# The fifth chunk of the keys as 15 block products, in pairs of half-width tiles, among the queries' products

## The chip, the core and the metric

One NeuronCore of a Trainium2 chip runs the whole kernel in one launch. The metric is device time in microseconds, the median of several runs. Everything is float32.

The engines are TensorE (PE in the profile, with its weight loads as PEld), VectorE (DVE), ScalarE (ACT), GpSimd (POOL) and SyncE (SP, which starts most DMAs). TensorE writes its products to PSUM, and VectorE and ScalarE read them from there. Each engine takes its own instructions in order and waits for the others by semaphores.

## The reference

A cross-attention block over 16 batches, each with 100 queries of width 640 and 718 keys of width 384 (plus four more tokens), in 8 heads of 80. Cut to what matters:

```
query = hidden_states @ Wq
keyt  = enc @ Wk
valt  = enc @ Wv
hs    = _mha(query, keyt, valt)              # softmax(q k^T / sqrt(80)) v, 8 heads
ca_hs1 = _mha(ca_q1, residual, residual)     # the four tokens' attention
ca_hs2 = _mha(ca_hs1 @ Wq, ca @ Wk_ca, ca @ Wv_ca)
out = (hs + ca_hs2) @ Wout + b_out + residual
```

The change concerns `keyt = enc @ Wk`: 718 keys from 384 inputs to 640 outputs. The 640 outputs stand in five chunks of 128 rows.

## The kernel before

**Batches.** `tile_xattn_kernel` loops over 16 batches. In turn `b` it finishes the attention of batch `b`, makes the values of `b` (`Values`, L410) and the keys of `b + 1` (`Keys`, L453), and prepares the second attention of `b + 1` and `b + 2` (`Second`, L854). Instructions are placed in the order of the program on each engine (`manual_schedule`). Parts that have steps of their own, `Keys`, `Values` and the softmax's `Maximum` (L785), are moved on by calls of `go(n)` in an order written by hand.

**Keys by 15 block products.** A product of 3 x 3 blocks by 3 x 2 blocks would take 18 block products. `Keys` and `Values` take 15: each multiplies a sum of input blocks by a sum of weight blocks, and the results collect in five accumulators A to E. After each product the accumulator is read and added to an output block, and the next product adds to the accumulator where it stands. `V_PLAN` and `K_PLAN` list (accumulator, form, output block); a form is the number of a pair of sums. The sums of the inputs are made on POOL for each batch (`enc_sums`, L481, 13 operations), those of the weights once (`weight_sums`, L502, 12 operations). The first write to an output block is a ScalarE copy (L407), later ones are VectorE additions (L405).

**The fifth chunk.** `Keys` makes chunks 0 to 3 of the 640 outputs in twos. The fifth, chunk 4, is left over and is made plainly: `last_keys` (L685) calls `chunk_keys` (L662), nine products of 128 x 128 weights with 240 columns each (L667), and two ScalarE copies (L678). It stands after the last block products of the turn, once VectorE has subtracted the maximum (`subtract(2)`, L1375) and ScalarE has the last exponential (L1383) in its queue.

**Queries.** Queries are made for two batches at a time, so in odd turns. In turns 3, 5, 7, 9, 11 and 13 the class `Queries` (L559) makes them by block products: `sums` puts six sums on POOL (L588), `make` (L607) first makes the fifth chunk of the queries (L626), then the others in pairs of column tiles of 64 (`product`, L590: weights of 64 columns, once for output partitions 0 to 63 and once for 64 to 127, matmul L594). Its accumulators a to e are read by ScalarE (L639, L647, L653, L655) and VectorE (L622). After it come the attention products (L1589), the products for the second attention (L875), and the next batch's scores (L710).

**Output pairs.** In five turns (last batch in `PAIRS`: turns 3, 6, 8, 11, 13) `project_pair` (L1144) makes two tiles of the output between `last_keys` and the queries. So turns 3, 11 and 13 have both, and turns 5, 7 and 9 have queries without an output pair (`parted`).

**The second attention** of four tokens runs beside this: `scores1` (POOL, L902 and L909), `softmax1` (a `Maximum` on VectorE; L801, L803, L806, L813, L831, L921), `scores2` (whose last step is L972 on POOL), `exponentials2` (ScalarE, L978), `softmax3`, `values2` (POOL, L1001 and L1008, token by token), and `keys` (POOL, L846), which masks the tokens' keys for `products` (L875).

**PSUM.** Three pools: `ps2` (two pairs of banks), `psk` and `ps1` (two banks each). `last_keys` took a pair from `ps2`.

**The largest of the scores** collects in `most`, a constant tile: 120 rows by `larger` (L1387, L1399), while rows 96 to 127 had been set to a low number once.

## Time and profile before

| | |
|---|---|
| median of 3 runs | 917.08 us (916.9 to 917.73) |
| the profiled execution's own time | 916.04 us |
| its span, first to last instruction | 914.1 us |
| granted TensorE clock | 1.000 |
| TensorE busy | 908.2 us, 99% |
| VectorE, ScalarE, POOL busy | 699.0, 434.2, 706.8 us |

The profile page gives busy time for each engine, groups of instructions by line, and waits; the timeline gives instructions in order of time, with the start, the length (of the whole row, where a row stands for several) and in brackets the idle time before and what ended it. A row such as `L594 ... x16` stands for 16 records. One float32 matmul leaves two records. TensorE's lengths overlap, since matmuls are pipelined: the time that a group takes is best read from its start to the start of the next.

### The profile page before, as it was taken

How to read it: one execution, taken by the hardware profiler on the slowest of the kernel's cores; microseconds unless marked ns; L12 is line 12 of the kernel's file. 1: busy time of each engine (PE TensorE's matmuls, PEld its weight loads, DVE VectorE, ACT ScalarE, POOL GpSimd, SP SyncE). 2: the span in 40 equal slices, each digit the busy share in tenths (PEclk: the TensorE clock that was granted, in tenths of full speed). 3: DMA queues.
4: the chain of work that ended last, by engine and by line, in shares of the span. 5: the costliest groups of instructions: out<-in, count | busy, mean ns of one | idle time of the engine just before them, and what ended most of it. 6: DMA issues, size and time to landing. Idle time of an engine off the chain costs nothing.

```text
span 914.1 us, 27711 instructions
## 1 busy us (share of the span) xinstructions
PE 908.2 (99%) x11962; PEld 762.8 (83%) x11962; DVE 699.0 (76%) x1126; ACT 434.2 (47%) x834; POOL 706.8 (77%) x672
## 2 busy tenths in 40 slices
PE   9999999999999999999999999999999999999998
PEld 6988889797797979888798787988879788797866
DVE  3669795989759897785967869679785897748883
ACT  2244543736337363652727436274741737427341
POOL 8577999787958879696896959958797697976623
PEclk9999999999999999999999999999999999999999
DMA  8822111131301212130121301103120031210111
GB/s 269 294 75 63 47 47 53 37 94 52 96 18 50 80 38 69 55 104 32 51 56 54 105 32 52 55 25 105 54 82 32 25 106 53 82 46 24 61 45 39
DMA packets 50582, 62.94 MB, mean 69 GB/s; under 512 B 13682, under 2 KB 37810, under 8 KB 50460
## 3 DMA queue, kind: packets, MB, share of 16 engines
q1 hardware_dynamic: 48812, 59.18, 21.2%
q8 instruction: 94, 1.54, 0.7%
q10 hardware_dynamic: 1024, 1.15, 0.4%
q0 software_dynamic: 624, 0.85, 0.3%
q14 instruction: 28, 0.23, 0.1%
HBM read 55.59 MB, written 5.57 MB: 67 GB/s over the span
## 4 chain that ended last, share of the span: by engine, by line
PE 96%; DVE 3%; ACT 0%; issue 0%; DVEq 0%
PE a_ps L1589 12%; PE s_ps L710 12%; PE v_psA L434 11%; PE v_psB L434 9%; PE k_psA L465 8%; PE k_psB L465 7%; PE kT_ps L667 6%; PE o_ps L1161 5%; PE v_psC L434 4%; PE k_psC L465 3%; PE q_ps L594 2%; PE q_ps L536 2%; PE v_psE L434 2%; PE v_psD L434 2%; PE v_ps L375 2%; PE q_psA L594 1%
## 5 line engine op out<-in xcount | busy, mean ns | idle before, releaser
L902 POOL TENSOR_TENSOR e<-ca,g 100x800 f32<-100x800 f32 x64 | 99.3, 1562 | 107.0 <-ACT kT L407 78.5
L500 POOL TENSOR_TENSOR enc<-enc 128x240 f32<-128x240 f32 x144 | 113.3, 797 | 14.7 <-DMA enc<-in_enct 7.5
L1375 DVE TENSOR_TENSOR st<-st,over 120x1600 f32<-120x1600 f32 x48 | 114.9, 2395 | 0.0
L1589 PEld LDWEIGHTS a_ps<-vs,st 120*36 120x36 f32 (+3 forms) x3072 | 109.3, 124 | 3.5 <-issue 3.4
L1589 PE MATMUL a_ps<-vs,st 120*36 120x81 f32 (+3 forms) x3072 | 111.7, 233 | 0.0
L434 PE MATMUL v_psA<-wv_sb,enc 128*120 128x320 f32 x352 | 109.3, 433 | 0.0
L1008 POOL TENSOR_TENSOR hs<-hs,hs 100x640 f32<-100x640 f32 x48 | 94.8, 1974 | 3.8
L1001 POOL TENSOR_TENSOR hs<-vb,p 100x640 f32<-100x640 f32 x64 | 91.1, 1434 | 8.4 <-issue 4.7
L465 PE MATMUL k_psA<-enc,wk_sb 128*128 128x240 f32 x384 | 95.3, 371 | 0.1
L909 POOL TENSOR_TENSOR e<-e,e 100x800 f32<-100x800 f32 x48 | 91.8, 1913 | 3.8
L434 PE MATMUL v_psB<-wv_sb,enc 128*120 128x320 f32 x296 | 91.8, 433 | 0.0
L1383 ACT ACTIVATE st<-st 120x1600 f32<-120x1600 f32 x48 | 73.9, 1539 | 32.3 <-DVE st L1375 31.8
L465 PEld LDWEIGHTS k_psA<-enc,wk_sb 128*128 128x128 f32 x384 | 71.5, 190 | 16.3 <-DVE wk_sb L522 0.5
L434 PEld LDWEIGHTS v_psA<-wv_sb,enc 128*120 128x120 f32 x352 | 64.2, 183 | 25.0 <-DVE vs L405 0.5
L1387 DVE TENSOR_TENSOR most<-most,st 120x800 f32<-120x800 f32 x64 | 66.3, 1036 | 15.9 <-ACT st L760 14.7
L465 PE MATMUL k_psB<-enc,wk_sb 128*128 128x240 f32 x320 | 78.0, 366 | 0.3 <-DVE sm L983 0.3
L710 PE MATMUL s_ps<-qp,kT 64*56 64x100 f32 (+1 forms) x3072 | 73.1, 248 | 0.0
L434 PEld LDWEIGHTS v_psB<-wv_sb,enc 128*120 128x120 f32 x296 | 54.1, 183 | 21.9 <-DVE vs L405 0.4
L710 PEld LDWEIGHTS s_ps<-qp,kT 64*56 64x56 f32 (+1 forms) x3072 | 66.9, 130 | 5.4 <-issue 4.2
L1076 ACT COPY hsT<-turned_hs 32x160 f32<-32x160 f32 (+7 forms) x244 | 67.7, 277 | 3.0
L465 PEld LDWEIGHTS k_psB<-enc,wk_sb 128*128 128x128 f32 x320 | 60.7, 190 | 8.6 <-issue 0.7
L766 ACT COPY st<-s_ps 120x800 f32<-120x800 f32 x64 | 49.8, 829 | 33.6 <-PE s_ps L710 33.6
(196 smaller groups left out, 1824.6 us busy)
## 6 DMA issues: line engine op xcount, KB each, us to landing
vb<-va_d SPq DMA_DIRECT2D x62, 250.0 KB
enc<-in_enct SPq DMA_DIRECT2D x30, 240.0 KB
enc<-in_enct SPq DMA_DIRECT2D x15, 360.0 KB
xT<-in_xt SPq DMA_DIRECT2D x8, 500.0 KB
rest<-in_enct SPq DMA_DIRECT2D x31, 120.0 KB
xn<-in_x SPq DMA_DIRECT2D x11, 320.0 KB
out<-xn SPq DMA_DIRECT2D x11, 320.0 KB
ca<-in_cas SPq DMA_DIRECT2D x16, 156.2 KB
```

Of the source, the lines that this page charges most:

```text
L434: nc.tensor.matmul(at[0][j][:KN, : H // 2], a_form(self.enc, f)[:, j * KN : (j + 1) * KN], wv_there.get(f, wv_sb[:, W_AT[f]]), start=first ...
L465: nc.tensor.matmul(at[:, i * KT : (i + 1) * KT], wk_sb[:, W_AT[f], i], a_form(self.enc, f), start=(first and i == 0), stop=last, skip_grou ...
L500: nc.gpsimd.tensor_tensor(out, left, right, op)
L710: nc.tensor.matmul(s_ps[at][k0:k1, cols], w, rhs, start=not begun & {(at, k) for k in range(k0, k1, 32)}, stop=last, skip_group_check=True,)
L902: first = nc.gpsimd.tensor_tensor(to, self.ca[:, t, :].unsqueeze(1).to_broadcast([S, NH, S]), g[:, :, t].unsqueeze(2).to_broadcast([S, NH, ...
L909: nc.gpsimd.tensor_tensor(e, e, to, ALU.add)
L1001: first = nc.gpsimd.tensor_tensor(to, self.vb[t][:S].rearrange("p (h d) -> p h d", h=NH), p2[:, :, t].unsqueeze(2).to_broadcast([S, NH, D] ...
L1008: nc.gpsimd.tensor_tensor(sums, sums, to, ALU.add)
L1076: nc.scalar.copy(self.hsT(r)[32 * m : 32 * m + 32, :, first - lo : end - lo], turned[32 * i : 32 * i + 32, :, m, first - at : end - at],)
L1375: return nc.vector.tensor_tensor(st[i], st[i], top.over[:KN].unsqueeze(1).to_broadcast([KN, 2, ROWS]), ALU.subtract,)
L1383: nc.scalar.activation(st[i], st[i], AF.Exp, scale=SCALE)
L1589: nc.tensor.matmul(a_v[lo:hi, h % 4], st[i // 2][: KEYS[i], i % 2, h * S + lo : h * S + hi], block(i, h // 4)[: KEYS[i], h % 4], start=(i ...
```

## The change

In turns 3, 5, 7, 9, 11 and 13 (`MIXED`) chunk 4 of the next batch's keys is no longer made by `last_keys`. A new class `Chunk` makes it by the same 15 forms, with weight blocks of 64 columns (`w4_form`: twelve sums in `w4_sums`, made by POOL in turn 1, and three blocks of `wk4` itself).

The products run in eight steps (`K4_PLAN`). Seven steps are a pair: two forms at a time, one to partitions 0 to 63 and one to 64 to 127, each streaming its own 240 input columns. One step is D alone, as two halves of 120 columns. A and B share one `ps1` bank, C, D and E another. After each step its two results are read: the first write to an output block by ScalarE, later ones by VectorE. The steps stand among the queries' products in `make`: two ahead, then one after each of the fifth chunk, a, b and so on.

With it go some moves. `softmax1` of these turns is cut into finer steps (`fine`) that stand between the queries' products or, where there is an output pair, between its products. The fourth token of `values2` and the masks `keys` move behind the queries' POOL step (the former already stood behind `sums` in turns 5, 7 and 9). `most` moves from a constant tile to one of the two `wide` buffers, and its rows from 96 on are set by a ScalarE copy in every batch.

```diff
+K4_PLAN = [
+    [("A", 7, (2, 1)), ("B", 13, (1, 0))],
+    [("D", 1, (2, 0))],
+    [("E", 6, (1, 0)), ("C", 12, (0, 1))],
+    [("A", 3, (2, 0)), ("B", 8, (2, 0))],
+    [("A", 9, (1, 0)), ("B", 10, (2, 1))],
+    [("A", 2, (0, 0)), ("B", 4, (0, 1))],
+    [("A", 0, (0, 1)), ("C", 11, (2, 1))],
+    [("A", 5, (1, 1)), ("B", 14, (0, 0))],
+]
...
         def make(self, tiles, chunk, between, freed):
...
+            chunk.go(2)
             for ch in range(HC):
...
+            between(2)
+            chunk.go()
             self.product(a, w(0, 0), v(0, 0), True)
             nc.scalar.copy(q(0, 0), full(a))
+            between(1)
+            chunk.go()
             self.rest(c, 0, 0, True)
             self.product(c, w(0, 1), v(1, 0), False)
+            between(1)
+            chunk.go()
             add(c, 0, 0)
             self.product(a, self.w2, self.t2, False)
             nc.gpsimd.tensor_tensor(self.w2, w(0, 1), self.w2, ALU.subtract)
+            freed()
+            between(1)
             self.rest(e, 1, 0, True)
+            chunk.go()
             self.product(e, w(1, 1), self.t4, False)
             nc.scalar.copy(q(1, 0), full(e))
+            chunk.go()
             add(a, 1, 0)
             self.product(b, self.w3, self.t3, True)
             add(b, 1, 0)
+            chunk.go()
             self.rest(d, 0, 1, True)
...
+    class Chunk:
+        def __init__(self, b, enc):
+            self.enc = enc
+            one, two = psum1(f"k4_psA_{b}"), psum1(f"k4_psC_{b}")
+            half = P // 2
+            self.at = {
+                "A": (one, 0, 0),
+                "B": (one, half, 0),
+                "C": (two, half, 0),
+                "D": (two, 0, KT),
+                "E": (two, 0, 0),
+            }
...
+        def go(self, n=1):
...
+                for bank, f, to, tile, k, lo, c0, n_cols in parts:
+                    nc.tensor.matmul(
+                        tile[k : k + half, lo : lo + n_cols],
+                        w4_form(f),
+                        a_form(self.enc, f)[:, c0 : c0 + n_cols],
+                        start=(bank, k) not in self.opened,
+                        stop=True,
+                        skip_group_check=True,
+                    )
+                    self.opened.add((bank, k))
+                for bank, f, (u, g), tile, k, lo, c0, n_cols in parts:
+                    out = kT[g * half : (g + 1) * half, HC - 1, u, c0 : c0 + n_cols]
+                    left = tile[k : k + half, lo : lo + n_cols]
+                    if (u, g, c0) in self.begun or (u, g, 0) in self.begun and c0 == 0:
+                        nc.vector.tensor_tensor(out, left, out, ALU.add)
+                    else:
+                        nc.scalar.copy(out, left)
+                    self.begun.add((u, g, c0))
...
+        most = wide(f"most_{b}")
+        nc.scalar.copy(most[96:], low[96:].to_broadcast([P - 96, ROWS]))
         st.append(scores(b, 0, tiles))
...
+            if b == 1:
+                weight_sums(nc.gpsimd, wk4)
             second.scores1(seen, range(T - 1))
...
-            last_keys(b + 1, enc)
+            if not mixed:
+                last_keys(b + 1, enc)
...
             else:
-                keys(m_next)
-                mixed.sums()
-                mixed.make(tiles, second.softmax1)
+                if last.b in PAIRS:
+                    second.softmax1()
+                    mixed.sums()
+                mixed.make(
+                    tiles,
+                    Chunk(b + 1, enc),
+                    second.softmax1,
+                    lambda: now.values2(None, later),
+                )
```

More of the change, by code (lines that the diff above doesn't have):

```diff
@@ L39 @@
 PAIRS = {ENDS[r + 1]: r for r in range(0, 10, 2)}
+MIXED = range(3, B - 1, 2)
 O_AFTER = [ENDS[r | 1] if r < 2 * len(PAIRS) else ENDS[r] for r in range(len(OC))]
@@ L123 @@
 NF = len(V_PLAN)
+W4_AT = {f: i for i, f in enumerate((0, 11, 12, 5, 7, 13, 1, 3, 6, 10, 2, 14))}
+W4_RAW = {9: (1, 1), 4: (2, 2), 8: (3, 1)}
 @with_exitstack
@@ L253 @@
     wk4 = const.tile([P, CC, P], F32, name="wk4")
+    w4_sums = const.tile([P, len(W4_AT), P // 2], F32, name="w4_sums")
     wq_sb = const.tile([P, HC, H], F32, name="wq_sb")
@@ L355 @@
     m_d = dram.tile([HC, P, B * HT], F32, name="m_d")
-    most = const.tile([P, ROWS], F32, name="most")
-    nc.gpsimd.memset(most[96:, :], LOW)
+    low = const.tile([P, 1], F32, name="low")
+    nc.gpsimd.memset(low, LOW)
     e1 = const.tile([P, ROWS], F32, name="e1")
@@ L500, in enc_sums, with w4, w4_form @@
             nc.gpsimd.tensor_tensor(out, left, right, op)
+    def w4(c, g):
+        return wk4[:, c - 1, (g - 1) * (P // 2) : g * (P // 2)]
+    def w4_form(f):
+        return w4(*W4_RAW[f]) if f in W4_RAW else w4_sums[:, W4_AT[f]]
     def weight_sums(engine, w, late=None, there={}):
@@ L506, in weight_sums @@
         raw = lambda c, g: w[:, 2 * (c - 1) + g - 1]
+        if w is wk4:
+            at, raw = w4_form, w4
         for f, left, right in (
@@ L605, in rest, with make @@
             self.product(bank, weights, self.xT[:, m, 4:], first)
-        def make(self, tiles, between):
+        def make(self, tiles, chunk, between, freed):
             qp, qz = tiles
@@ L692, in last_keys @@
         )
+    class Chunk:
[10 more added lines that the diff above has]
+            }
+            self.plan = iter(K4_PLAN)
+            self.opened, self.begun = set(), set()
+        def go(self, n=1):
+            half = P // 2
+            for _, step in zip(range(n), self.plan):
+                parts = []
+                for bank, f, to in step:
+                    tile, k, lo = self.at[bank]
+                    if len(step) > 1:
+                        parts.append((bank, f, to, tile, k, lo, 0, KT))
+                        continue
+                    for i in range(2):
+                        parts.append((bank, f, to, tile, i * half, lo, i * KN, KN))
+                for bank, f, to, tile, k, lo, c0, n_cols in parts:
[16 more added lines that the diff above has]
+                    self.begun.add((u, g, c0))
     def scores(b, g, tiles):
@@ L785, with __init__ @@
     class Maximum:
-        def __init__(self, top, name, scalar=False):
-            self.name, self.scalar = name, scalar
+        def __init__(self, top, name, scalar=False, fine=False):
+            self.name, self.scalar, self.fine = name, scalar, fine
             self.step = self.steps(top)
@@ L808, in steps @@
                 )
+            if self.fine:
+                yield
             mx = small.tile([P, NB], F32, tag="mx", name=f"mx_{name}")
@@ L818, in steps @@
                 )
-            yield
+                if self.fine and lo == 32:
+                    yield
+            if not (self.fine and scalar):
+                yield
             spread = wide(f"spread_{name}").rearrange("p (b k) -> p b k", k=32)
@@ L911, in scores1, with softmax1 @@
                     wait_for(first, behind)
-        def softmax1(self, n=8):
+        def softmax1(self, n=9):
             if not self.top:
-                self.top = Maximum(e1, f"1_{self.b}", self.b - 2 in PAIRS)
+                self.top = Maximum(
+                    e1, f"1_{self.b}", self.b - 2 in PAIRS, self.b - 1 in MIXED
+                )
             if self.top.over is not None:
@@ L1142, in sums, with project_pair @@
                 nc.gpsimd.tensor_tensor(out, left, right, op)
-        def project_pair(self):
+        def project_pair(self, between):
             r = PAIRS[self.b]
@@ L1174, in project_pair @@
             product(b1, [(one[:, :2], w(0, 0))], True)
+            between(1)
             read(b1, 0, 0)
+            between(1)
             product(b2, [(one[:, 2:4], w(1, 0)), (one[:, 4:], last(0))], True)
@@ L1182, in project_pair @@
             nc.gpsimd.tensor_tensor(wout2[:, 0], wout2[:, 0], w(0, 0), less)
+            between(2)
             product(b4, [(two[:, 2:4], wout2[:, 1])], True)
@@ L1482 @@
                 last.sums()
-            parted = b % 2 and b > 1 and last.b not in PAIRS
-            now.values2(None, range(T - 1 if parted else T))
+            later = range(T - 1, T) if b in MIXED else range(0)
+            now.values2(None, range(T - len(later)))
             vv.go(2)
@@ L1501 @@
             mixed = None
-            if b % 2 and b > 1:
+            if b in MIXED:
                 second_next, enc_next = loads()
                 mixed = Queries(p + 1, xT_at[0], enc_next[0])
-            if parted:
-                mixed.sums()
-                now.values2(None, range(T - 1, T))
+                if last.b not in PAIRS:
+                    mixed.sums()
             if b == 1:
@@ L1521 @@
             if last.b in PAIRS:
-                second.softmax1(3)
-                last.project_pair()
+                if not mixed:
+                    second.softmax1(3)
+                last.project_pair(second.softmax1 if mixed else lambda n: None)
                 if last.b == max(PAIRS):
@@ L1528 @@
                     )
-            second.softmax1(3 if parted else 8)
+            if not mixed:
+                second.softmax1(8)
         else:
@@ L1561 @@
                     queries(p + 1, xT, tiles, n)
-            elif parted:
-                mixed.make(tiles, second.softmax1)
-            else:
-                keys(m_next)
-                mixed.sums()
-                mixed.make(tiles, second.softmax1)
+            else:
+                if last.b in PAIRS:
+                    second.softmax1()
+                    mixed.sums()
+                mixed.make(
[3 more added lines that the diff above has]
+                    lambda: now.values2(None, later),
+                )
         if 0 < b < B - 2:
-            if not mixed or parted:
-                keys(m_next)
+            keys(m_next)
             enc_sums(enc_next)
```

## The prediction

> **What bounds the kernel now.** I read first the page's busy times (share of the span, number of instructions).

> ```profile
> PE 908.2 (99%) x11962; PEld 762.8 (83%) x11962; DVE 699.0 (76%) x1126; ACT 434.2 (47%) x834; POOL 706.8 (77%) x672
> ```

> TensorE works almost without a gap, so a microsecond of products taken away is won, and a microsecond that TensorE waits is lost for good: no idle time further on absorbs it. The question is what the change takes from TensorE and which waits it puts in. The timeline of batch 5 (start, length, engine), cut to the place of the change, shows what is taken.

> ```profile
> 348.74 1.38 PE L667 MATMUL kT_ps<-enc,wk 128*128 128x240 f32 x6
> ...
> 352.48 1.91 PE L626 MATMUL q_ps<-xT,wq_sb 128*64 128x200 f32 x20
> ...
> 354.22 0.86 PE L594 MATMUL q_psA<-xT,wq_sb 128*64 128x100 f32 x16
> ...
> 354.90 1.20 PE L594 MATMUL q_ps<-xT,wq_sb 128*64 128x100 f32 x24
> ...
> 355.94 0.86 PE L594 MATMUL q_psA<-enc 128*64 128x100 f32 x16
> ```

> The fifth chunk (L667) runs from 348.74 to 352.48: 3.74 us for nine products of 240 columns (the trace has two records for each product). I take 0.09 of it for the passage to tiles of 64, which stays (L626's five pairs of 200 columns take 1.74 where L594's rate, below, gives 1.70). That leaves 3.65, or 0.405 a product.

> **TensorE's own gain.** Eight steps take its place: seven pairs of 240 columns and one pair of 120. L594 is made of such pairs: 16 records are four pairs of 100 columns, and 354.90 less 354.22 is 0.68, so 0.17 for 100 columns and 0.41 for 240. Seven of these and one half are 3.09 us (3.04 at L667's rate). In L594 both halves of a pair stream the same rows; in the new pairs they don't. One place of the old kernel has pairs with two different streams:

> ```profile
> 875.28 2.91 PE L1207 MATMUL o_ps<-wout_sb,hsT 128*64 128x320 f32 x20
> ```

> Five pairs of 320 columns in 2.91 us are 0.58 a pair; one after the other they would be 1.08 (320 columns at 0.405 for 240, twice). They overlap. The gain is 3.65 - 3.09 = 0.56 us a batch, 3.4 us over six.

> **What each step waits for.** The two old copies of the result become 16 reads: seven copies on ScalarE and nine additions on VectorE. A and B lie in one PSUM bank, and each step adds to what the step before left there, so it can't start until both reads of that one are done. The built order of after.py has these waits: step A9/B10 waits for B8's addition, A2/B4 for B10's, A0/C11 for B4's, which itself waits for A2's copy on ScalarE, and A5/B14 for A0's. Behind the waiting product stand the queries' products, and behind these the attention's. Prices and hand-overs, from the groups of instructions and the timeline:

> ```profile
> L678 ACT COPY kT<-kT_ps 128x240 f32<-128x240 f32 x16 | 5.8, 364 | 0.0
> ```
> ```profile
> 356.22 0.37 DVE L622 TENSOR_TENSOR qp<-q_ps,qp 128x200 f32<-128x200 f32 x1 [2.72 <-PE q_ps L594]
> ...
> 357.65 0.86 PE L594 MATMUL q_psB<-enc 128*64 128x100 f32 x16
> 357.87 0.33 ACT L647 COPY qp<-q_ps 128x200 f32<-128x200 f32 x1 [2.42 <-PE q_ps L594]
> ...
> 361.94 0.63 DVE L622 TENSOR_TENSOR qp<-q_psA,qp 128x200 f32<-128x200 f32 x2
> ```
> ```profile
> 79.63 0.65 DVE L405 TENSOR_TENSOR kT<-k_psB,kT 128x480 f32<-128x480 f32 x1
> ...
> 80.43 0.64 PE L465 MATMUL k_psB<-enc,wk_sb 128*128 128x240 f32 x2 [0.34 <-DVE sm L983]
> ```
> ```profile
> 347.63 1.81 DVE L1375 TENSOR_TENSOR st<-st,over 120x1600 f32<-120x1600 f32 x1
> ...
> 349.54 1.54 ACT L1383 ACTIVATE st<-st 120x1600 f32<-120x1600 f32 x1
> ...
> 352.58 0.82 ACT L678 COPY kT<-kT_ps 128x480 f32<-128x480 f32 x2 [1.51 <-PE kT_ps L667]
> ```

> A copy of 240 columns takes 0.36. An addition lies between 0.37 (200 columns, L622) and 0.65 (480, L405): about 0.40 by the line through the two; two in a row overlap by 0.1 (L622: 0.63 for two). From the start of TensorE's next group to the waiting copy pass 0.22 (357.65 to 357.87), to the addition 0.28 (355.94 to 356.22), between VectorE and ScalarE 0.10 (349.44 to 349.54), and back to TensorE 0.15 (80.28 to 80.43), of which I take 0.10, between none and this. The cover is TensorE's own work between the steps: 1.04 for 24 records (354.90 to 355.94), 0.69 for 16.
> - A3/B8 to A9/B10, and on to A2/B4: 0.28 + 0.71 + 0.10 = 1.09 against 1.04: 0.05 lost, twice.
> - A2/B4 to A0/C11: copy, then addition, 0.22 + 0.36 + 0.10 + 0.40 + 0.10 = 1.18 against 0.69: 0.49 lost.
> - A0/C11 to A5/B14: 0.28 + 0.40 + 0.10 = 0.78 against 0.69: 0.09 lost.

> That is 0.68 us in each of the six batches, somewhat more than the gain of 0.56. C12's copy also waits for E6's addition, with the copy of q(0, 0) behind it, which is needed only two steps later.

> A2's copy and B4's addition, which wait for each other here, read different halves of the bank. [...]

> **The batches without an output pair (5, 7, 9).** Here ScalarE is late too. D's two halves must be copied before E6/C12 may start in their bank, and ScalarE works in order. Its exponential (349.54, above) starts when VectorE's subtraction ends and is done at 351.08, whatever TensorE does. Behind it stand the copies of A7, B13 and D's halves: 0.27, 0.27, 0.15 and 0.25 (overlapping by 0.1, as the two of L678 do; 0.25 for 120 columns is an estimate from 0.36 at 240 and 0.33 at 200). They end at 352.0, and E6/C12 may start at 352.1. TensorE is there at 348.74 + 0.41 + 0.21 + 1.74 (L626) = 351.1. Lost: 1.0 us. Such a batch comes to -0.56 + 0.68 + 1.0 = +1.1. In batches 3, 11 and 13 the pair's output products stand between and cover the exponential; they come to +0.1. Six batches: 3.6 us.

> **The twelve weight sums on POOL in batch 1.** They are small, but they stand ahead of the second attention's scores, where POOL is already late:

> ```profile
> 112.44 3.04 POOL L902 TENSOR_TENSOR e<-ca,g 100x800 f32<-100x800 f32 x2
> ...
> 120.99 0.24 POOL L972 TENSOR_TENSOR e<-s,mx 100x32 f32<-100x32 f32 x1
> ...
> 121.27 0.23 ACT L978 ACTIVATE e<-e 100x32 f32<-100x32 f32 x1 [7.72 <-POOL e L972]
> 121.40 0.74 ACT L407 COPY vs<-v_psC 120x320 f32<-120x320 f32 x2
> ...
> 122.47 1.24 PE L434 MATMUL v_psC<-wv_sb,enc 128*120 128x320 f32 x4
> ```

> L902's row names no idle time: POOL comes to it straight from other work. L972 stands behind it on POOL, the exponential L978 waits for L972 (ScalarE idles 7.72 us), and the copies of v_psC, for which the product at 122.47 waits, stand behind L978. They end at 122.14, 0.3 us ahead of it. The sums have 128x64 elements; the nearest row is

> ```profile
> 358.24 1.41 POOL L846 TENSOR_TENSOR m<-mb,hmask 128x64 f32<-128x64 f32 x5
> ```

> 0.28 each, 3.4 us in all (at 0.24, as L972, 2.9; a tenth above L846, 3.8). The product moves to 122.14 + 3.4 + 0.1 = 125.6: 3.2 us lost, once (2.7 to 3.6). What follows moves together on all engines.

> **What is hidden.** The constant rows of `most` now come by a ScalarE copy of 32x800 ahead of the score copies, of some 0.8 (L766 has 800 columns a copy).

> ```profile
> 266.96 0.37 ACT L893 COPY y_sb<-y_ps 100x256 f32<-100x256 f32 x1 [8.65 <-DVE g L889]
> 267.87 1.55 ACT L766 COPY st<-s_ps 120x800 f32<-120x800 f32 x2 [0.54 <-PE s_ps L710]
> ...
> 370.58 1.55 ACT L766 COPY st<-s_ps 120x800 f32<-120x800 f32 x2 [1.15 <-PE s_ps L710]
> ```

> Where ScalarE idles 1.15 us before L766 the copy is free; where it idles 0.54, as after batch 3, the score copies move by 0.3, which I take as 0.1 lost in 3, 11 and 13, 0.2 to 0.3 in all. `most` takes turns in the two `wide` buffers; the one that it gets is free once the second softmax's last transpose is done, before the attention products end. The mask products `keys` (L846, 1.41), moved behind the queries in batches 3, 11 and 13, are first read after the attention products (L1589); the fourth token's product and addition after half of these. Without that cover TensorE would wait for their length, 1.4 us for `keys`. The second softmax's steps change places with VectorE's reads, where its queue idles (2.72 us before L622). No DMA is added, and the rest of the keys' inputs is loaded at the same place.

> **The sum.** 3.6 + 3.2 + 0.2 = 7.0 us. On the profiled execution (span 914.1, its own time 916.04) that is 923.0; on the median of the three runs, 917.08, it is 924.1. The two differ by 0.1%, and I forecast against the median. About 0.2% (1.8 us) can be told from no change. Ends: losses of 0.4 (no time back to TensorE) to 1.4 us (every restart 0.15 dearer) in each of the six batches, 0.8 to 1.2 more in 5, 7 and 9, and batch 1's 2.7 to 3.6 give 4 to 12.5 us.

> **Rivals.**
> - *Faster: the reads are hidden.* If a bank's round trip (L760 to the next L760) stays under TensorE's work between, and the sums don't make L972 late, the 3.4 us of gain are left: 913.7. It decides at 0.69 us for A2/B4 to A0/C11. For it: nothing else on VectorE is late. Against it: copy and addition alone are 0.76. Chance 0.05.
> - *Hidden reads, but batch 1 waits*: 917.08 - 3.4 + 3.2 = 916.9, no change. 0.08.
> - *Only the six batches lose*, because the sums find POOL idle: 920.9. Against it: L902 has no idle time before it in batch 1. 0.13.
> - *Dearer restarts*: each of five waits costs TensorE a further 0.15: 924.1 + 6 x 0.75 = 928.6. 0.10.
> - *The pairs run one after the other*: another 3.1 us a batch, 943. L1207 speaks against it. 0.02.

> The built order holds the 15 products in all six batches, so the change does what it says. My forecast has 0.62. Faster is 0.05; no change takes the second rival and a little of the low end of mine, 0.09; slower 0.86. From 918.0 to 928.5 leaves out the first, second and last rival and half of the fourth.

> **What would show it.** In the profile after: TensorE idle before L760, about 0.5 before A0/C11 in all six batches and 1 us before E6/C12 in batches 5, 7 and 9 alone; a gap of 3 us before v_psC near 122.5; ScalarE's wait for L972 near 11 us; L760's steps at 0.41 us. It would be wrong if those gaps are missing, or if a gap stands elsewhere: before the attention products, or at the scores.

## The result, and the profile after

| | before | after |
|---|---|---|
| median of 5 runs | 917.13 us (916.9 to 918.16) | 925.53 us (923.84 to 926.31) |
| the profiled execution's own time | 916.04 us | 925.86 us |
| its span | 914.1 us | 924.1 us |
| its mean granted TensorE clock | 1.000 | 0.998 |

The ratio is 1.0087, with an interval from 1.0072 to 1.0101: slower by 8.4 us on the medians, where 7.0 were forecast. The page's busy times:

```profile
PE 910.4 (99%) x12046; PEld 757.5 (82%) x12046; DVE 716.3 (78%) x1180; ACT 457.2 (49%) x880; POOL 709.0 (77%) x684
```

The span grew by 10.0 us. TensorE's busy time took 2.2 of them (908.2 to 910.4); 7.8 are time in which it waits. The waits of TensorE alone (line, what was waited for: total, times, longest):

```profile
PE k_psC L760 <- ACT kT L775: 3.1, 3, 1.0
PE v_psC L450 <- ACT vs L423: 2.9, 1, 2.9
PE k_psA L760 <- DVE kT L773: 1.3, 6, 0.2
```

Three waits of 1.0 before E6/C12 (tile k_psC), one of 2.9 in batch 1, and six of 0.2 before A0/C11. None of them is in the profile of before. Batch 5 in the timeline, from the chunk's first step to the attention products:

```profile
353.35 0.63 PE L760 MATMUL k_psA<-enc,w_sums 128*64 128x240 f32 x4
353.80 0.38 PE L760 MATMUL k_psC<-enc,w_sums 128*64 128x120 f32 x4
354.01 1.86 PE L651 MATMUL q_ps<-xT,wq_sb 128*64 128x200 f32 x20
356.92 0.63 PE L760 MATMUL k_psC<-enc,w_sums 128*64 128x240 f32 x4 [1.04 <-ACT kT L775]
...
358.46 1.20 PE L618 MATMUL q_ps<-xT,wq_sb 128*64 128x100 f32 x24
359.61 0.42 PE L760 MATMUL k_psA<-enc,wk 128*64 128x240 f32 x1
...
361.62 0.85 PE L618 MATMUL q_ps<-enc,wq_sb 128*64 128x100 f32 x16
362.70 0.42 PE L760 MATMUL k_psA<-enc,w_sums 128*64 128x240 f32 x1 [0.23 <-DVE kT L773]
...
363.16 0.86 PE L618 MATMUL q_psB<-enc 128*64 128x100 f32 x16
363.85 0.60 PE L760 MATMUL k_psA<-enc,w_sums 128*64 128x240 f32 x4
...
366.33 0.87 PE L1691 MATMUL a_ps<-vs,st 120*64 120x81 f32 x20
```

Starts tell more than the idle time in brackets, since lengths overlap. From 361.62 to 362.70 are 1.08 for products that take 0.69 (363.16 to 363.85): A0/C11 loses 0.39. Products of 24 records take 1.15 up to A9/B10 (358.46 to 359.61) for 1.03: 0.12 lost. The whole piece takes 12.98. Before, it took 11.66, from 348.74 to the start of the attention products:

```profile
360.40 6.94 PE L1589 MATMUL a_ps<-vs,st 120*64 120x81 f32 x192
```

The last key products ahead of the piece take 0.09 more than before (352.44 to 353.35, against 347.93 to 348.74).

Batch 1 in the timeline:

```profile
112.19 1.15 POOL L546 TENSOR_TENSOR w_sums<-wk 128x64 f32<-128x64 f32 x4
...
115.76 3.04 POOL L990 TENSOR_TENSOR e<-ca,g 100x800 f32<-100x800 f32 x2
...
124.55 0.23 ACT L1068 ACTIVATE e<-e 100x32 f32<-100x32 f32 x1 [11.19 <-POOL e L1062]
124.69 0.73 ACT L423 COPY vs<-v_psC 120x320 f32<-120x320 f32 x2
125.15 1.53 PE L450 MATMUL v_psC<-wv_sb,enc 128*120 128x320 f32 x4 [2.85 <-ACT vs L423]
126.47 2.34 PE L450 MATMUL v_psB<-wv_sb,enc 128*120 128x320 f32 x4
...
128.61 1.45 PE L481 MATMUL k_psB<-enc,wk_sb 128*128 128x240 f32 x4
```

The sums run on GpSimd from 112.19 to 115.76, 3.57 us, and the chain L1062, L1068, copies, v_psC is as late as forecast. What was not forecast stands in the two last rows: the four records of v_psB take 2.14 from start to start, the double of the 1.07 of before:

```profile
123.55 1.24 PE L434 MATMUL v_psB<-wv_sb,enc 128*120 128x320 f32 x4
124.62 0.97 PE L465 MATMUL k_psB<-enc,wk_sb 128*128 128x240 f32 x4
```

The table of stretches gives the clock (length, busy times of PE, PEld, DVE, ACT and POOL, then the granted clock):

```profile
127.00:128.00 1.00, 1.00 (x3) 0.65 (x2) 1.00 (x2) 0.21 (x1) 1.00 (x1) 0.50 0.00 0
...
130.00:131.00 1.00, 1.00 (x7) 0.86 (x6) 1.00 (x1) 0.56 (x1) 1.00 (x1) 1.00 0.00 0
```

From 6.69 to 126.16 the clock is 1.00. Shortly after the wait it falls to 0.50, from 126.16 to 129.57, and comes back. From v_psC to v_psA (125.15 to 130.71) pass 5.56 us, before 3.77 (122.47 to 126.24): 1.8 more.

To place losses I compare, in each kernel, the start of the second attention's products y_ps, which stand behind the attention products of every batch, with their start in the profile of before. For batch 6:

```profile
424.20 0.92 PE L875 MATMUL y_ps<-m,xT 128*36 128x72 f32 x20
```
```profile
430.12 0.93 PE L963 MATMUL y_ps<-m,xT 128*36 128x72 f32 x20
```

that is 5.92 us late. The table has the lateness after batch 0, and what each later stretch added (us; "5" is from behind batch 3 to behind batch 5, and so on). The kernels are those of the experiments below.

| kernel | 0 | 1 | 3 | 5 | 7 | 9 | 11 | 13 |
|---|---|---|---|---|---|---|---|---|
| after | -0.34 | 4.80 | 0.10 | 1.38 | 1.85 | 1.52 | 0.23 | 0.01 |
| sums_batch2 | 0.66 | 0.00 | 0.10 | 1.27 | 1.41 | 2.07 | 0.22 | 0.09 |
| exp_late | -0.10 | 3.31 | 1.23 | 0.17 | 0.12 | 0.24 | 0.27 | 0.09 |
| step_later | 1.77 | 2.86 | -0.16 | 1.17 | 1.13 | 0.96 | -0.28 | -0.31 |
| reduce_later | 0.06 | 4.48 | 0.10 | 1.97 | 2.03 | 2.35 | 0.15 | 0.09 |
| banks | 1.60 | 2.94 | 0.22 | 0.93 | 1.31 | 1.60 | 0.07 | -0.07 |
| all_three | 1.78 | -0.01 | 0.38 | -0.05 | -0.12 | -0.11 | -0.29 | -0.52 |
| all_three_again | 1.66 | 0.15 | -0.35 | -0.45 | 0.15 | 0.10 | -0.23 | -0.35 |
| before_sums12 | 3.44 | 4.38 | 0.52 | 0.55 | -0.01 | 0.19 | 0.38 | 0.29 |
| before_sums8 | 0.37 | 1.97 | 0.26 | 0.09 | 0.00 | 0.00 | -0.03 | 0.19 |
| old_chunk | 0.72 | 0.11 | 0.13 | 0.80 | 0.00 | 0.00 | 0.27 | 0.12 |
| before_again | 1.62 | -0.01 | 0.00 | 0.66 | -0.01 | 0.19 | 0.54 | 0.64 |

The last row is the old kernel itself in a second execution. It shows how far one cell can be trusted: gaps of 0.2 to 0.7 us, and one of 1.2 in batch 0, come and go between executions of the same kernel.

### The profile page after: what moved, and what is told of

The parts are those of the page before. It is cut to its first block, busy times and chain, and to the rows that moved or that the text cites. A ratio compares the mean times of both kernels' runs of the same rounds, so it can differ in the third digit from the quotient of the medians.

```text
span 924.1 us, 27985 instructions
## 1 busy us (share of the span) xinstructions
PE 910.4 (99%) x12046; PEld 757.5 (82%) x12046; DVE 716.3 (78%) x1180; ACT 457.2 (49%) x880; POOL 709.0 (77%) x684
## 3 DMA queue, kind: packets, MB, share of 16 engines
q10 hardware_dynamic: 1024, 1.15, 0.4%
## 4 chain that ended last, share of the span: by engine, by line
PE 89%; POOL 4%; DVE 4%; ACT 2%; issue 1%; DMA 1%; ACTq 0%; POOLq 0%; DVEq 0%
PE a_ps L1691 11%; PE s_ps L793 11%; PE v_psA L450 10%; PE v_psB L450 9%; PE k_psA L481 8%; PE k_psB L481 6%; PE o_ps L1251 5%; PE v_psC L450 3%; PE kT_ps L703 3%; PE k_psC L481 3%; PE q_ps L560 2%; PE k_psA L760 2%; PE v_psD L450 2%; PE v_psE L450 2%; PE q_ps L618 1%; PE v_ps L391 1%
## 5 line engine op out<-in xcount | busy, mean ns | idle before, releaser
L990 POOL TENSOR_TENSOR e<-ca,g 100x800 f32<-100x800 f32 x64 | 99.2, 1560 | 94.6 <-ACT kT L423 54.7
L516 POOL TENSOR_TENSOR enc<-enc 128x240 f32<-128x240 f32 x144 | 115.7, 814 | 14.3 <-PE q_ps L560 5.3
L793 PE MATMUL s_ps<-qp,kT 64*64 64x100 f32 (+1 forms) x3072 | 73.1, 248 | 0.0
L793 PEld LDWEIGHTS s_ps<-qp,kT 64*64 64x64 f32 (+1 forms) x3072 | 66.9, 130 | 5.4 <-issue 4.2
L423 ACT COPY vs<-v_psA 120x640 f32<-120x640 f32 x45 | 31.2, 693 | 66.6 <-PE v_psA L450 66.4
```

The costliest lines, as they stand in the source:

```text
L516: nc.gpsimd.tensor_tensor(out, left, right, op)
L793: nc.tensor.matmul(s_ps[at][k0:k1, cols], w, rhs, start=not begun & {(at, k) for k in range(k0, k1, 32)}, stop=last, skip_group_check=True,)
L990: first = nc.gpsimd.tensor_tensor(to, self.ca[:, t, :].unsqueeze(1).to_broadcast([S, NH, S]), g[:, :, t].unsqueeze(2).to_broadcast([S, NH, ...
```

## The experiments

The kernel before, run beside the experiments, had medians of 918.3 to 918.7 us, so ratios are compared, and times only with that in mind.

**The weight sums in batch 2 (sums_batch2).**

```diff
-            if b == 1:
+            if b == 2:
                 weight_sums(nc.gpsimd, wk4)
```

> The twelve weight sums are issued in batch 2 instead of batch 1, the rest is the changed kernel (925.5 us). My theory: in batch 1 they cost 4.4 us, 2.7 of TensorE's wait for v_psC (2.85 idle, less what the row before moved) and 1.8 because the granted clock is 0.50 in the 2.2 us after that wait. In batch 2 GpSimd idled 5.7 us ahead of the second attention's scores, the sums take 3.6. So 921.1 us, no gap before v_psC, granted clock 1.00 there, and no new gap in batch 2. Rival (a): the low clock has another cause and stays: 922.8. Rival (b): GpSimd is late in batch 2 as well and the wait only moves: 924 to 926, with TensorE idle before a v_ps product of batch 2.

Ratio 1.0058 (1.0038 to 1.0078), median 923.55 us. The interval holds the forecast (921.1 of 917.1 is 1.0044), rival (a) and the lower end of rival (b), and the runs scatter from 921.64 to 926.85; the trace decides. The timeline of batch 1, then GpSimd's of batch 2:

```profile
123.13 1.24 PE L450 MATMUL v_psC<-wv_sb,enc 128*120 128x320 f32 x4
124.21 1.24 PE L450 MATMUL v_psB<-wv_sb,enc 128*120 128x320 f32 x4
```
```profile
159.27 3.48 POOL L546 TENSOR_TENSOR w_sums<-wk 128x64 f32<-128x64 f32 x4
...
165.49 1.16 POOL L546 TENSOR_TENSOR w_sums<-wk 128x64 f32<-128x64 f32 x4
166.60 3.04 POOL L990 TENSOR_TENSOR e<-ca,g 100x800 f32<-100x800 f32 x2
```

No gap before v_psC, full rate behind it, and batch 1 adds 0.00 instead of 4.80. In batch 2 the lateness stays at 0.66. So the sums' whole price comes from their place. They were not shorter there: in batch 2 the twelve take 7.4 us (159.27 to 166.65) and not 3.6, the first four 3.48 instead of 1.15, for a reason that the runs don't show. The scores behind them (L990) start at 166.60, where they started at 164.40 before, and TensorE waits for nothing.

**The third exponential later in turns 5, 7 and 9 (exp_late).** (In this kernel, and in the one with the three edits together, lines are two higher: L777 is the copy, L775 the addition, L762 the product.)

```diff
             subtract(2)
-            exponential(2)
+            if not mixed or last.b in PAIRS:
+                exponential(2)
...
             nc.scalar.copy(q(0, 0), full(a))
+            if late:          # lambda: exponential(2) in turns 5, 7, 9
+                late()
```

> In turns 5, 7 and 9 ScalarE's third exponential is issued behind the copy of the first query product, where ScalarE idled 3.04 us, instead of ahead of the fifth chunk's copies; the sums stay in batch 1. My theory: the three gaps of 1.04 us before E6/C12 go, so 925.5 - 3.1 = 922.4 us (922.1 to 922.6). Rival: the gap is the copies' own round trip and the bank, not the exponential ahead of them; then it stays at 0.8 to 1.0 us and the time at 925 to 925.5. A second rival: the exponential is then late for the attention products, 1 to 1.5 us each, and the time stays near 925.5 with TensorE idle before these.

Ratio 1.0051 (1.0033 to 1.0069), 0.36% less than after, or 3.3 us. ScalarE and TensorE in batch 5:

```profile
353.95 0.72 ACT L777 COPY kT<-k_psA 64x240 f32<-64x240 f32 x2
354.68 0.52 ACT L777 COPY kT<-k_psC 64x120 f32<-64x120 f32 x2
...
357.35 1.54 ACT L1478 ACTIVATE st<-st 120x1600 f32<-120x1600 f32 x1
```
```profile
355.63 0.57 PE L762 MATMUL k_psC<-enc,w_sums 128*64 128x240 f32 x4
```

D's copies are done 0.4 us before TensorE comes to E6/C12, and the three waits are gone from the list. Turns 5, 7 and 9 add 0.17, 0.12 and 0.24. The exponential is hidden at its new place: nothing waits ahead of the attention products. (The 1.23 of turn 3 in this execution is a gap of 0.4 at an output product and one behind z_ps.)

**The last two steps one product later (step_later).**

```diff
             nc.scalar.copy(q(1, 0), full(e))
-            chunk.go()
             add(a, 1, 0)
             self.product(b, self.w3, self.t3, True)
             add(b, 1, 0)
             chunk.go()
             self.rest(d, 0, 1, True)
             self.product(d, self.w2, v(1, 1), False)
+            chunk.go()
```

> The last two steps (A0/C11 and A5/B14) are each issued one query product later; nothing else changes. My theory: A0/C11 lost 0.39 us a batch because copy and addition of A2/B4 come one after the other in one bank and only 0.69 us of products stood between; with 1.37 us between, nothing is lost, and A5/B14 has 1.03 us for 0.78. So 925.5 - 6 x 0.39 = 923.2 us. Rival: the last reads then come late and the wait moves to the queries' last copies, the attention or the scores: 925 to 927.

Ratio 1.0059 (1.0045 to 1.0074), 0.28% less than after, or 2.6 us. The six waits before A0/C11 are gone and nothing takes their place; the six turns together add 2.5 us instead of 5.1 (4.6 without a gap of 0.45 behind z_ps in turn 7, which belongs to that execution).

**Copy or reduction (reduce_later).** In after, a reduction of the second softmax (L898) ends at 362.21 on VectorE and ScalarE's copy of A2 at 362.19; B4's addition starts at 362.24. Which did it wait for?

```diff
             freed()
-            between(1)
             self.rest(e, 1, 0, True)
             chunk.go()
             self.product(e, w(1, 1), self.t4, False)
             nc.scalar.copy(q(1, 0), full(e))
             chunk.go()
+            between(1)
```

> The changed kernel with one step of the second softmax (VectorE's reduction of 32x100, two halves, 0.67 us) moved from ahead of A2/B4's addition to behind A0/C11's. In the changed kernel this reduction and ScalarE's copy of A2 end within 0.02 us of each other (362.21 and 362.19), so the trace doesn't tell which of them B4's addition waited for. If it was the copy (my prediction's step), the addition starts as before, 0.05 us behind the copy, and A0/C11 still loses 0.35 to 0.4 us: ratio 1.008 to 1.009. If it was the reduction, the addition starts some 0.3 us earlier, beside the copy, A0/C11 loses 0.1 us, and the ratio is 1.0055 to 1.0065.

Ratio 1.0125 (1.0105 to 1.0144). ScalarE and VectorE in batch 5:

```profile
361.98 0.35 ACT L775 COPY kT<-k_psA 64x240 f32<-64x240 f32 x1 [3.04 <-PE k_psA L760]
```
```profile
362.37 0.41 DVE L773 TENSOR_TENSOR kT<-k_psA,kT 64x240 f32<-64x240 f32 x1 [0.72 <-ACT kT L775]
```

With nothing ahead of it on VectorE, the addition waits 0.72 us, until 0.04 after the copy's end: it was the copy, and A0/C11 still loses 0.38. The time was expected by neither: at its new place the reduction is ahead of the queries' additions, and TensorE waits for these (three waits for L646 of together 1.0 before q_psB; turns 5, 7 and 9 add 0.2 to 0.8 more than in after). The profile shows 1.7 us more than after; the ratio, 0.4% above that of after, is twice as much, and that half I can't place, except that five of the six runs had a mean clock of 0.995 to 0.997.

**Other banks (banks).**

```diff
-                "B": (one, half, 0),
-                "C": (two, half, 0),
-                "D": (two, 0, KT),
+                "B": (two, half, 0),
+                "C": (one, half, 0),
...
+            chunk.at["D"] = (b, 0, 0)
             chunk.go(2)
...
             add(b, 1, 0)
-            chunk.go()
             self.rest(d, 0, 1, True)
             self.product(d, self.w2, v(1, 1), False)
+            chunk.go()
```

Here `b` is the bank of the queries' accumulator b, which they use later.

> The changed kernel with another place in PSUM for three of the five accumulators: B and C change banks, so that A2 and B4 lie in different banks, and D lies in the bank that the queries use later; A0/C11 stays where it was, A5/B14 is issued one product later (else it would wait for both additions of A0/C11). The sums stay in batch 1 and the exponential ahead of the copies. My theory: what A0/C11 lost (0.39 us) is the copy of A2 and the addition of B4 one after the other because both read one bank; side by side they leave A0/C11 only the copy, 0.68 us against 0.69 of products, so the 0.4 us go, as in the run with both steps later: ratio 1.006 to 1.0065 against 1.0087 of the changed kernel (some 2.3 us less), and VectorE's addition of B4 starts while ScalarE copies A2. Rival: VectorE or ScalarE comes late to these reads for another reason, and A0/C11 still waits 0.3 to 0.4 us: ratio 1.008 to 1.009.

Ratio 1.0065 (1.0049 to 1.0081). Batch 5 in the timeline:

```profile
356.76 0.42 PE L760 MATMUL k_psC<-enc,w_sums 128*64 128x240 f32 x1 [0.53 <-ACT kT L775]
...
361.77 0.87 PE L618 MATMUL q_ps<-enc,wq_sb 128*64 128x100 f32 x14
362.45 0.37 PE L760 MATMUL k_psA<-enc,w_sums 128*64 128x240 f32 x1
```
```profile
361.97 0.35 ACT L775 COPY kT<-k_psA 64x240 f32<-64x240 f32 x1 [3.23 <-PE k_psA L760]
...
362.57 0.41 DVE L773 TENSOR_TENSOR kT<-k_psC,kT 64x240 f32<-64x240 f32 x1
```

A0/C11's first product starts at 362.45, when ScalarE's copy is done and before B4's addition has begun: it no longer waits for it. In batch 5 the addition began no earlier than before, because the reduction (L898) stands ahead of it. In batch 3 nothing does, and there the addition starts while the copy runs, as expected:

```profile
258.33 0.35 ACT L775 COPY kT<-k_psA 64x240 f32<-64x240 f32 x1 [3.23 <-PE k_psA L760]
```
```profile
258.52 0.41 DVE L773 TENSOR_TENSOR kT<-k_psC,kT 64x240 f32<-64x240 f32 x1 [0.39 <-PE k_psC L760]
```

Batches 11 and 13 show the same, and in all six turns B14's addition overlaps A5's copy. In after, with both in one bank, the addition of batch 3 waited 0.71 for the copy's end, and in none of the one-bank kernels does an addition of 240 columns overlap a copy of 240. So the shared bank is what puts one behind the other in the built program. E6/C12 waits 0.53 instead of 1.04, since two copies fewer stand behind the exponential, and A3/B8 waits 0.37 (at 358.44) for C12's copy, which now shares its bank.

**The three edits together (all_three, all_three_again).**

> The three edits together: sums in batch 2, the third exponential later in turns 5, 7 and 9, the last two steps one product later. If the three losses are separate they add up: 925.5 - 4.4 - 3.1 - 2.3 = 915.7 us, 1.4 below the kernel before, that is, the 3.4 us that TensorE saves less some 0.2 a batch for the two remaining short waits and 0.5 elsewhere. Rival: what is late next takes their place (VectorE's additions, or the second attention on GpSimd), and the time stays at 918 to 920.

Ratio 0.9980 (0.9969 to 0.9990), median 916.66 us.

> The three edits together once more, for a second interval on another set of executions: ratio 0.998 as the first time (0.997 to 0.999). In the profile, each of the six turns should be 0.3 to 0.4 us shorter than in the kernel before from the start of the fifth chunk to the attention products, with no wait of TensorE longer than 0.2 us between them. If the first ratio was an accident of the executions, it is 1.000.

Ratio 0.9964 (0.9950 to 0.9978), median 915.65 us against 918.68 of the kernel before. Both intervals end below 1: this version is faster than the kernel before, by 0.2 to 0.4%. Batch 5 in the second profile:

```profile
350.15 0.63 PE L762 MATMUL k_psA<-enc,w_sums 128*64 128x240 f32 x4
350.61 0.38 PE L762 MATMUL k_psC<-enc,w_sums 128*64 128x120 f32 x4
350.81 1.86 PE L651 MATMUL q_ps<-xT,wq_sb 128*64 128x200 f32 x20
352.50 0.57 PE L762 MATMUL k_psC<-enc,w_sums 128*64 128x240 f32 x4
...
361.40 1.79 PE L1695 MATMUL a_ps<-vs,st 120*64 120x81 f32 x46
```

11.25 us from the first step to the attention products, 0.41 less than the 11.66 of before. Some 0.09 of it reappears ahead of the chunk, where the passage to narrow tiles now lies, so 0.32 a batch are won, as expected (0.3 to 0.4). No wait of TensorE in it is longer than 0.2. Over the six turns the two profiles show -0.7 and -1.1 us in the table, less than six times 0.32, because of single gaps between the turns, as in the last row of the table.

**The old kernel with the sums alone (before_sums12, before_sums8).** Twelve or eight subtractions of 128x64 on GpSimd in batch 1; their results are overwritten unused.

```diff
+            if b == 1:
+                for i in range(12):          # or 8
+                    nc.gpsimd.tensor_tensor(
+                        wout2[:, i // 10, i // 5 % 2, i % 5 * 64 : i % 5 * 64 + 64],
+                        wk4[:, i % 3, :64],
+                        wk4[:, (i + 1) % 3, 64:],
+                        ALU.subtract,
+                    )
             second.scores1(seen, range(T - 1))
```

> The kernel before with twelve subtractions of 128x64 on GpSimd at the place in batch 1 where the change put its weight sums; their results are overwritten unused, and nothing else of the change is in it. My theory: GpSimd is late there by itself, so the price is that of batch 1 in the changed kernel: twelve times 0.30 is 3.6 us on GpSimd, of which TensorE's product for v_psC waits 2.7 to 3.3, and 0 to 1.8 more where the clock falls to one half behind that wait. Ratio to the kernel before 1.003 to 1.005. Rival: in the old order GpSimd has slack ahead of the second attention's scores, and it costs nothing (1.000).

Ratio 1.0050 (1.0036 to 1.0063). A wait of 2.44 before v_psC, then the clock:

```profile
128.50 2.43 PE L434 MATMUL v_psC<-wv_sb,enc 128*120 128x320 f32 x4 [2.44 <-ACT vs L407]
```
```profile
130.00:131.00 1.00, 1.00 (x3) 0.59 (x2) 1.00 (x2) 0.00 (x0) 1.00 (x1) 0.50 0.00 0
```

> The same with eight subtractions, 2.4 us on GpSimd. If GpSimd's lateness is passed on one to one, the wait for v_psC is 1.2 us shorter than with twelve: 1.5 to 2.1 us, ratio 1.0016 to 1.0023, and a wait of this length leaves the granted clock at 1.00. If a shorter wait lowers the clock too, 1.5 us more.

Ratio 1.0020 (1.0010 to 1.0030):

```profile
124.41 1.34 PE L434 MATMUL v_psC<-wv_sb,enc 128*120 128x320 f32 x4 [1.42 <-ACT vs L407]
125.59 1.24 PE L434 MATMUL v_psB<-wv_sb,enc 128*120 128x320 f32 x4
```

Four subtractions fewer are 1.1 us less on GpSimd (2.23 for 3.35) and 1.02 less wait, and the products behind it run at full rate. Batch 1 costs 4.38 and 1.97 us. GpSimd's lateness is passed on almost one to one, without any other part of the change. Both waits are somewhat shorter than expected (2.7 to 3.3 and 1.5 to 2.1); both ratios lie in their ranges.

**The moves alone (old_chunk).** The changed kernel with `last_keys` in place of `Chunk`, and without the weight sums.

> The changed kernel with the old fifth chunk (nine products of 128 columns' tiles, two copies) in turns 3 to 13, ahead of the output pair as before, and without the weight sums: only what the change moved is left, that is, the constant rows written by ScalarE in every batch, the steps of the second softmax among the queries' products, the mask products and the fourth token's product behind them. My theory prices all this at 0.2 to 0.5 us: ratio 1.0000 to 1.0006. Rival: the moves cost by themselves, up to 0.3 us in each of the six turns, and 1.8 us in all (1.002).

Ratio 0.9999 (0.9990 to 1.0007): the moves cost nothing that can be measured, as forecast (0.2 us).

**The kernel before once more (before_again).**

> The kernel before, unchanged, for a second profiled execution beside the others on their chip. If the gap of 1.1 us at k_psA in batch 0 and the gaps of 0.2 to 0.5 us behind z_ps, which the experiments showed and the first profile of before did not, belong to single executions and not to the change, some of them show here too, and the span is 914 to 917. If they belong to the changed kernel, none does, and the span is 914.1 again.

Span 917.7 us, a little above the range. TensorE's waits:

```profile
PE z_ps L931 <- issue: 1.3, 3, 0.6
PE k_psA L465 <- DVE kT L405: 1.2, 1, 1.2
```

Both kinds of gap are in the old kernel too. They belong to single executions.

## Why the prediction was right, and where not

Forecast 924.1 us, measured 925.53; the sum was 7.0 us, measured 8.4 on the medians and 9.8 on the own times of the two profiled executions. The cause named was the cause: the reads of the chunk's results and the sums on GpSimd; with their waits removed by order alone the loss is gone (all_three). Of the rivals "the reads are hidden" is excluded by the waits in all six turns, "only the six batches lose" (920.9) by before_sums12, "the pairs run one after the other" by steps of 0.40 us; of "dearer restarts" a third is there, 0.05 for 0.15.

- **TensorE's own gain, 0.56 a batch: mechanism right, size too large.** The two halves of a pair overlap: a step without a wait takes 0.40 us (forecast 0.41). But the first step, and each behind a wait, takes 0.45, which the sum left out: the eight steps of after take 3.30 and not 3.09. In all_three_again, where waits of 0.12 and 0.06 are left, 0.32 us a batch are won.
- **A2/B4 to A0/C11, 0.49: mechanism right, size 0.39.** The addition does wait for the copy (reduce_later), TensorE for the addition, because the two accumulators share a bank (banks), and time between the steps hides it (step_later). I took 0.22 + 0.36 + 0.10 + 0.40 + 0.10 from the start of the products between; measured in batch 5 are 0.22 + 0.35 + 0.05 + 0.41 + 0.05 = 1.08. The two hand-overs were half as long as I took them. Copy and addition read different halves of the bank; within one bank the built order kept them apart in every trace (in batch 3 of after the addition waits 0.71), so what they do side by side there is not shown. With two banks the wait is gone.
- **The other steps.** A9/B10 and A2/B4 lost 0.12 and 0.07 (forecast 0.05 each), A5/B14 nothing (0.09).
- **Turns 5, 7 and 9, +1.1 each: +1.38, +1.85 and +1.52 in the table.** Turn 7 has the gap of 0.45 in it, so they come to 1.4 each. D's copies behind the exponential are shown as the cause by exp_late. The term of 1.0 is too small by about 0.2, as much as the dearer steps add: from L651's start to E6/C12 pass 2.91 us, where 1.69 do without a wait (350.81 to 352.50), so 1.2 are lost and not 1.0. The copies began when the exponential ended, 355.62, and took 1.24, where I had 0.9.
- **Turns 3, 11 and 13, +0.2 each with the copy of the constant rows: +0.10, +0.23 and +0.01.** Right within what single executions show.
- **Batch 1, 3.2 us: right for the wait, and the step that failed is "what follows moves together on all engines".** Where the clock stayed up, batch 1 cost 3.31, 2.86 and 2.94 (exp_late, step_later, banks). Where it fell, 4.80, 4.48 and 4.38 (after, reduce_later, before_sums12). TensorE's own rate behind a long wait was missing from the sum. In the two profiled executions the six turns add 5.1 for a forecast of 3.8, and batch 1 4.8 for 3.2, which is about the 2.8 between 7.0 and 9.8. How much of the 8.4 on the medians is the clock stays open: of the five runs after, only the profiled one (mean clock 0.998) is known to hold the fall; the median run had 0.999, as had the profile of sums_batch2, which holds none before its last product. In exp_late the three runs at 1.000 took 921.28 to 921.57 us, the three at 0.997 to 0.998 took 923.49 to 925.15.
- **What is hidden: right.** old_chunk prices all of it at nothing.

## What to carry to other kernels

Where TensorE is the bound, a saving of half a microsecond per batch is lost to one badly placed read (1.2 us before E6/C12 here): before splitting a product into accumulating pieces, list for each piece which engine reads it, what stands ahead of that read in the engine's queue, and how much of TensorE's work lies between. Work done once also wants a queue with room: the same twelve sums on GpSimd cost about 3 us of the whole in batch 1, more where the clock fell, and nothing in batch 2. And such losses are repaired by order alone; three moves of lines turned 0.9% slower into 0.2 to 0.4% faster.

## What the runs showed of the hardware

Behind three waits of TensorE its granted clock stood at 0.50 for 3.41 us: one of 2.85 us (after, 126.16 to 129.57), of 2.74 (reduce_later, 125.05 to 128.46) and of 2.44 (before_sums12, 128.59 to 132.01). Behind waits of 2.75 (exp_late), 2.37 (banks) and 2.30 us (step_later) it stayed at 1.00, as behind 1.42 (before_sums8) and 1.04 (after). Batch 1 cost 4.38 to 4.80 us in the three where it fell and 2.86 to 3.31 in the three of 2.30 to 2.75 where it stayed: some 1.5 us between them (1.8 from v_psC to v_psA in after). The length alone doesn't decide it. The stretch of exp_late that answers to the one at 0.50 above:

```profile
127.00:128.00 1.00, 1.00 (x6) 0.81 (x5) 1.00 (x2) 0.08 (x1) 1.00 (x1) 1.00 0.00 0
```

It holds six records of products, that of after three.
